# A list scheduler counts all transfers as one pipe instead of fixed landing times

## Chip, cores and metric

The kernel runs on one NeuronCore of one Trainium2 chip. The metric is the device time of one execution in microseconds (us); lower is better. The time before is 2759.6 us, the median of three runs (2759.0 to 2762.83).

## What is computed

The input x holds 32 graphs ("batches") of 512 nodes with 256 features in float32; one 512 x 512 adjacency matrix is shared by all. Four layers follow one another, each a graph attention on a layer-normed input, added to x:

```python
h = relu(layernorm(x)); x = x + elu(gat(h, adj, W0, a0, alpha=0.2))          # layer 0
h = relu(layernorm(x)); x = x + relu(gat(h, adj, W1, a1, alpha=0.01))        # layer 1
h = relu(layernorm(x)); x = x + elu(gat4(h, adj, W2, a2, alpha=0.2))         # layer 2: 4 heads of 64
h = relu(layernorm(x)); x = x + L3(h)                                        # layer 3
...
def gat(h, mask, W, a, alpha):
    v = h @ W
    e = leaky_relu(v @ a1[:, None] + (v @ a2)[None, :], alpha)   # 512 x 512
    return softmax(where(mask, e, -inf)) @ v
...
def L3(h):
    o = relu(h @ mlp1_w + mlp1_b)                     # 512 wide
    o = elu(elu(gat(o, None, W_fc, a_fc, 0.2))) + o   # no mask
    r = relu(o @ mlp2_w + mlp2_b)                     # 256 wide
    return relu(elu(elu(gat(r, adj, W_hand, a_hand, 0.2))) + r)
```

## The kernel before

**Work of one batch.** All 512 nodes of a batch lie on chip as four tiles of 128 rows. A layer norms x (`norm`, L653 to L664, on VectorE/DVE and ScalarE/ACT), transposes the result on TensorE/PE (`turn_pair`, L442; ACT takes it out as hT, L674) and multiplies with the weights (`values`, L434 W,hT). The attention weights are exp of a maximum of two sums, so they are built as a product form: a row of exp terms is brought onto all partitions, and DVE makes each 128 x 512 block of w with one instruction (`weights`, L737: maximum with a column, times the mask). The row goes to DRAM (`rows_out`: PE transpose, ACT copy L749, store "row" L751 on SP's queue) and comes back spread over the partitions (`spread`, L757, 256 KB, three buffers). PE then sums w times v (`aggregate`, L434 v,w), DVE takes a reciprocal (L769), ACT and DVE finish.

Layer 2 has four heads: four spreads, sixteen w, and column-tiled matmuls (L438, three groups of 32 per batch) between transposes. Layer 3 has no mask in its first attention, so for batches 0 to 30 it is computed by sorting (`sort_attend`): DVE and ACT count each node's place (L1003, L1016), POOL writes rows to their places in DRAM with indirect transfers ("order", L1025), SP reads them back ("sums", L1036), DVE and PE make running sums (L1048 to L1070), SP writes them to a table in DRAM (L1071, 1032 KB), and POOL gathers one row per node ("g", L1079); DVE combines them (L1093), ACT and DVE apply elu twice (L1096, L1097, L796 to L798), PE transposes, DVE adds into oT (L1152). The last batch multiplies directly (`attend`). The output is added on POOL (L1137) and stored (L1138).

**Streams.** Four streams (NS = 4) hold batches i, i+4, i+8 and so on. Each is a generator that yields a planner time, `after_us(us)`, which is its step's begin plus STRETCH times the step's PE cycles plus SLOW times the given us. The loop at the end of `fast` always lets the stream with the smallest time go on. Stream i begins at i * LEAD plus an offset; in its first batch it also waits PAUSES[3b + layer] after each of its first three layers. The setup (mask, products of the weights, triangles) is a fifth generator of twelve pieces, written out at a fixed distance. This fixes only the order in which the program is written down, which is each instruction's rank.

**Planner.** The program is built twice. The first time `jobs_of` finds all dependencies, `price` gives each instruction an assumed duration, and `in_order` makes a list schedule: on each engine, of the instructions that are ready by the assumed times, the one of the lowest rank goes next. A tile's buffers and the eight PSUM banks are given out in the same run. The second time the instructions are held in that order on each engine (`arrange`), so an engine whose next instruction waits does nothing else. The assumed durations appear nowhere in the program; the waits on the chip are those of the data.

For a transfer, `price` sets `took` (from issue to landing), `flux` (time in the one shared pipe) and `holds` (the issuing engine). In `in_order` a transfer with a flux is done when the pipe has taken it:

```python
clock[e], done = at + job.holds, at + job.took
if job.flux:
    done = array["pipe"] = max(done, array["pipe"]) + job.flux
```

Before the change only the loads of the kernel's inputs (names that begin with in_) have a flux, at 350 GB/s, x of batches 4 and up excepted. All others land after a fixed time, whatever else is under way: 5.6 us for sums, 4.3 for a spread plus 0.9 for each further head, 6.5 for the table, 6.8 for g, 4.1 for order, 2.6 for a row.

Of the kernel before, what the change touches and what calls it, by code (L numbers as in the profile page):

```python
# [67 lines left out]
class Job:  # L68
# [9 lines left out]
HANDOVER = {"PE": 40.0, "DVE": 33.0, "Activation": 33.0, "Pool": 70.0, "SP": 28.0}  # L78
LANDING = {
    "sums": 5600.0, "spread": 4300.0, "table": 6500.0, "x": 10000.0, "order": 4100.0, "g": 6800.0, "out": 4500.0,  # L80
    "adj": 9000.0,
}
SHORT = {"table": 5200.0, "row": 2600.0, "out": 4500.0}
SWITCH = 93.0
# [25 lines left out]
def price(job, outs, ins, in_psum):  # L110

    e, op = job.engine, job.op
    if op == "Matmult":
        (name, _, moving), (_, _, still) = ins[0], ins[1]
        turned = name.startswith("ident")
        job.span = P if turned else int(job.ins.tile_size[1])
        whole = str(list(job.ins.ins)[1].dtype).endswith("float32")
        job.passes = 2 if whole and not turned else 1
        job.rest, job.fills = [], outs[0][0]
        job.load = 109.0 * elements(still) / P * job.span / P  # L120
        job.flow = 109.0 if turned else (elements(moving) * (5.0 / 6.0 if whole else 0.45) + 2.4) * job.span / P
        return
    n = max(elements(s) for _, _, s in outs + ins) if outs + ins else 1
    wide = [name for name, _, s in ins if elements(s) > 48]
    columns = sum(1 for _, _, s in ins if elements(s) == 1) if n > 48 else 0
    if op == "DMACopy":
        name, _, s = outs[0]
        kind = name.split("_")[0].rstrip("0123456789")
        large = elements(s) * s[0][1] > 5000
        job.took = LANDING.get(kind, 6000.0) if large else SHORT.get(kind, 3300.0)  # L130
        if kind == "spread":
            job.took += 900.0 * (ins[0][1] // 512)
        if ins[0][0].startswith("in_") and not (kind == "x" and ins[0][1] >= 4 * 512 * 256):
            job.took, job.flux = 2500.0, max(160.0, 4.0 * elements(s) * s[0][1] / 350.0)
        job.holds = (2000.0 if kind == "order" else 1290.0) if e == "Pool" else 600.0 if kind in ("sums", "table") else 400.0
        return
    if e == "DVE":
        if op == "BNStats":
            t = 409.0
        elif n <= 48:  # L140
            t = 158.0 + n
        elif op in ("TensorTensor", "TensorReduce") or len(wide) > 1:
            t = 155.0 + 1.042 * n + (55.0 * columns if op == "TensorScalarPtr" else 0.0)
        elif any(map(in_psum, wide)):
            t = 205.0 + 1.045 * n
        else:
            t = 205.0 + 0.43 * n + 45.0 * columns
        job.holds = max(45.0, t - 84.0)
    elif e == "Activation":
        if n <= 48:  # L150
            t = 170.0 + n + 90.0 * (len(ins) > 1)
        elif any(map(in_psum, wide)):
            t = 170.0 + 0.82 * n + 90.0 * min(columns, 1)
        else:
            t = 200.0 + 0.84 * n + 85.0 * min(columns, 1)
        job.holds = max(60.0, t - 100.0)
    else:
        t = 1271.0 if op == "TensorTensor" and n > 48 else 250.0
        job.holds = t
    if len(outs) > 1:  # L160
        job.holds, t = job.holds + 85.0, t + 165.0
    job.took = t
# [238 lines left out]
def fast(ctx, tc, plan, flag, x, adj, w0, a0, w1, a1, w2, a2, mlp1_w, mlp1_b, mlp2_w, mlp2_b,  # L401
# [9 lines left out]
    NS = 4  # L411
    LEAD = 81.69
    GO = 7.0
    PAUSES = (1.98, 20.79, 0, 9.87, 13.42, 5.98, 12.87, 2.43, 0, 28.8, 13.7, 0)
    SLOW = 1.53
    STRETCH = 1.75

# [258 lines left out]
    def turned(xn, when):  # L676
# [4 lines left out]
        turn_pair(xn, hT, 2)  # L681
        yield after_us(0.26)
        return hT
# [8 lines left out]
    def values(hT, w, rs=None):  # L692

        v = work.tile([P, NT, F + 3], FP, tag="v", name="v", bufs=4)
        for t in range(NT):
# [14 lines left out]
            if t + 1 < NT:  # L710
                yield after_us(0.32)
        yield after_us(0.7)
        return v

    def linear_t(inT, w, bias, name, bufs):
# [3 lines left out]
        for f in range(ft):  # L719
# [3 lines left out]
            nc.scalar.activation(o[:, f, :], p, AF.Relu, bias=bias[:, f:f + 1])  # L723
            yield after_us(0.05 if f == ft - 1 else 2.73)
        return o
# [46 lines left out]
    def plain(hT, w, rs=None, far=False):  # L772
        v = yield from values(hT, w, rs)
        r = None
        if far:
            r = spread(rows_out(v[:, :, F + 2], 1)[0, :])
            yield after_us(11.34)
        wt = weights(lambda t: v[:, t, F + 2:F + 3], lambda j: v[:, j, F + 1:F + 2], r=r)
        note(v[:, :, F:])
        yield after_us(0.41)  # L780
        return v, wt
# [18 lines left out]
    def layer0(xt, xn, rs, when):  # L800
        v, wt = yield from plain((yield from turned(xn, when)), W0, far=True)
        xn, rs = new_xn(), small([NT], "rs")
        for t0 in range(0, NT, 2):
            r, q = pair(), pair("q")
            for i in range(2):
# [3 lines left out]
                if i == 0:  # L809
                    yield after_us(0.56)  # L810
            add_elu(xt[:, t0:t0 + 2, :], r, q)
            norm(xt, xn, rs, t0, True)
            last, when = when, after_us(0.48)
            if t0 == 0:
                yield after_us(0)
        yield last
        return xn, rs, when

    def layer1(xt, xn, rs, when):
        v, wt = yield from plain((yield from turned(xn, when)), W1, rs, far=True)  # L820
        xn, rs = new_xn(), small([NT], "rs")
        for t0 in range(0, NT, 2):
            r = pair()
            for i in range(2):
                p, rd = averages(v, wt, t0 + i)
                nc.scalar.activation(r[:, i, :], p, AF.Relu, scale=rd)
                if i == 0:
                    yield after_us(3.06)
            xr = xt[:, t0:t0 + 2, :]
            nc.vector.tensor_tensor(xr, xr, r, op=OP.add)  # L830
            norm(xt, xn, rs, t0, True)
            last, when = when, after_us(1.98)
            if t0 == 0:
                yield after_us(0.04)
        yield last
        return xn, rs, when

    def layer2(xt, xn, rs, when):
        hT = yield from turned(xn, when)
        v = work.tile([P, NT, NH, CH], FP, tag="v", name="v2", bufs=4)  # L840
        for t in range(NT):
# [10 lines left out]
            )  # L852
            yield after_us(1.87 if t + 1 < NT else 0.3)
        row_d = rows_out(v[:, :, :, D + 2], NH)
# [3 lines left out]
        def begin():  # L858
# [3 lines left out]
            )  # L862
            return after_us(0.05)

# [5 lines left out]
        )  # L870
        yield after_us(14.86)
        begin()
        note(v.rearrange("p t h c -> p (t h) c")[:, :, D:])
        yield after_us(0.87)
        when = begin()
        for g, parts in enumerate(plan):
# [9 lines left out]
            nc.scalar.copy(s, p)  # L886
            yield after_us(1.08)
            if g < 2:
# [23 lines left out]
            if g:  # L912
# [3 lines left out]
                add_elu(xt[:, :, (g - 1) * 2 * D:g * 2 * D], y, q)  # L916
            yield after_us(3.1)
        xn, rs = new_xn(), small([NT], "rs")
        for t0 in range(0, NT, 2):
            norm(xt, xn, rs, t0, False)  # L920
        yield after_us(4.83)
        return xn, rs, after_us(1.14)

# [27 lines left out]
    def attend(oT, b):  # L951

        halves, ends = fc_values()
        for c in range(2):
            for t in range(NT):
                project_half(oT, halves, ends, c, t)
                yield after_us(0.48)
            if c == 0:
                nc.gpsimd.tensor_copy(halves[0][:, :, F:], ends[:, :, :2])
                note(ends)  # L960
        wt = weights(lambda t: ends[:, t, 2:3], lambda j: ends[:, j, 1:2], masked=False)
        yield after_us(0.73)
        ys = []
        for t in range(NT):
# [9 lines left out]
            ys.append(y)  # L974
            yield after_us(0.14)
            if t:
                mlp_in(oT, ys[t - 1], t - 1)
                yield after_us(0.1)
        yield after_us(0)
        mlp_in(oT, ys[-1], NT - 1)  # L980
        yield after_us(0)

    def sort_attend(oT, b):
# [6 lines left out]
        for t in range(NT):  # L990
            project_half(oT, halves, ends, 0, t)
            yield after_us(1.43)
        project_half(oT, halves, ends, 1, 0)
        yield after_us(0.78)
        for c in range(2):
            nc.gpsimd.tensor_copy(halves[c][:, :, F:], ends[:, :, :2])
        tj = spread(rows_out(ends[:, :, 1], 1)[0, :])
        yield after_us(5.75)

# [8 lines left out]
        note(ends)  # L1008
        sort = after_us(3.88)
        yield after_us(0.32)  # L1010
        for t in range(1, NT):
            project_half(oT, halves, ends, 1, t)
            yield after_us(3.04)
        for t in range(NT):
# [6 lines left out]
        for c in range(2):  # L1021
# [14 lines left out]
            for read in (nc.sync.dma_start(u, rows), nc.sync.dma_start(flat[c][:, 2, :], rows[:, 0, :])):  # L1036
                for other in placed:
                    tc.add_manual_dep(read.ins, other.ins.name, landed, reason="rows of four tiles")
            sort = after_us(0.46)
        places = table[:N, :].rearrange("(p t) (k c n) -> p (t k) c n", t=NT, k=2, c=2)  # L1040
        sort = after_us(0.54)
        for c in range(2):
# [11 lines left out]
            for t in (2, 1, 0):  # L1054
                nc.vector.scalar_tensor_tensor(  # L1055
                    u[:, t, :], u[:, t, :], T[:, t:t + 1], u[:, t + 1, :], op0=OP.mult, op1=OP.add
                )
            yield after_us(1.92)

# [12 lines left out]
            nc.sync.dma_start(table[N:, c * C:(c + 1) * C], tot[P - 1:, :])  # L1072
            sort = after_us(6.33)
        yield after_us(12.5)
        got, when, gs = [], [], []
# [10 lines left out]
        gather(1)  # L1086
        landed = after_us(9.82)
        for t in range(NT):
# [12 lines left out]
            got.append(y)  # L1101
            landed = after_us(0.46)
            when.append(after_us(12.63))
            if t == 0:
# [4 lines left out]
        mlp_in(oT, got[-1], NT - 1)  # L1109
        yield after_us(0.11)  # L1110

    def layer3(xt, xn, when, b):
# [6 lines left out]
        for t0 in range(0, NT, n):  # L1119
# [21 lines left out]
            if t0 == 0 and b + NS < B:  # L1141
                first_norm(b + NS)
            yield after_us(0)

# [21 lines left out]
    def batch(b):  # L1166
        if b < NS:
            first_norm(b)
            yield after_us(20.8)
        else:  # L1170
            yield after_us(0.8)
        xt, xn, rs = normed.pop(b)
        when = after_us(2.46)
        for i, layer in enumerate((layer0, layer1, layer2)):
# [14 lines left out]

    ready = {i: i * LEAD + late for i, late in enumerate((0, 4.35, 4.97, 5.59))}  # L1190
    streams = [stream(i) for i in range(NS)]
    early = setup()
    ready[NS] = 1.42
    while ready:
        i = min(ready, key=ready.get)
        if i == NS:
            turn[0] = NS - 1
            ready[i] += 19.61
            if next(early, early) is early:
# [463 lines left out]
```

## Time and profile before

| | before |
|---|---|
| runs (us) | 2759.0, 2759.6, 2762.83 |
| profiled execution | 2780.08 us, its span 2778.3 us |
| granted TensorE clock, mean | 0.993 |
| PE, DVE, ACT, POOL busy in the span (us) | 2711.2, 2288.7, 1625.7, 515.4 |
| bytes moved | 314.04 MB, mean 113 GB/s |
| matmuls and weight loads | 13944 each |

The profile is of one execution. Times in it are from the span's start. "A <- B" in the waits means that A was held up until B was done; a chain lists what released what, back from the last instruction. Matmuls overlap one another, so their busy times are those of the union, and the mean of one is longer than its share.

### The profile page before, as it was taken

The page shows a single profiled execution, that of the slowest core. Times are in us where ns is not written, and L with a number is a line of the kernel's source. Part 1 is how long each engine was busy: PE and PEld are TensorE (multiplying, and loading weights), DVE is VectorE, ACT ScalarE, POOL GpSimd, SP SyncE. Part 2 cuts the span into 40 slices and gives each one's busy share as a digit, 9 for nine tenths or more (in the row PEclk, how much of TensorE's full clock was granted, in tenths as well). Part 3 has the DMA queues.
Part 4 walks back from the last instruction along what each step waited for, and adds up shares of the span by engine and source line. Part 5 has one row for each costly group of instructions (what it writes and reads, how often), then busy time and mean ns, then how long its engine had stood idle before and what let it go on. Part 6 is the DMA issues. An engine that isn't in the chain of part 4 may idle for free.

```text
span 2778.3 us, 41413 instructions
## 1 busy us (share of the span) xinstructions
PE 2711.2 (98%) x13944; PEld 1906.2 (69%) x13944; DVE 2288.7 (82%) x5889; ACT 1625.7 (59%) x4228; POOL 515.4 (19%) x516
## 2 busy tenths in 40 slices
PE   5999999999999999999999999999999999999998
PEld 4666677766767676676767667676676766777655
DVE  5788888888878889788897888978989789888875
ACT  3455666566556565555765566655665556565554
POOL 0012221212112221012221222111221112212120
PEclk8999999999999999999999999999999999999999
DMA  4033333334424343144341434423443234333331
GB/s 129 24 103 113 125 122 103 122 107 134 137 77 133 122 132 123 60 136 138 126 134 60 126 131 133 131 69 113 147 136 109 89 115 138 126 102 114 116 131 37
DMA packets 214885, 314.04 MB, mean 113 GB/s; under 512 B 17356, under 2 KB 156934, under 8 KB 214664
## 3 DMA queue, kind: packets, MB, share of 16 engines
q1 hardware_dynamic: 184904, 213.01, 24.8%
q0 software_dynamic: 29760, 98.30, 10.3%
q8 instruction: 112, 1.84, 0.3%
q14 instruction: 109, 0.89, 0.1%
HBM read 195.61 MB, written 115.65 MB: 112 GB/s over the span
## 4 chain that ended last, share of the span: by engine, by line
PE 69%; DVE 23%; ACT 5%; issue 1%; DMA 1%; SPq 0%; another core or an unknown queue 0%; DVEq 0%
PE b L434 54%; PE b L438 8%; PE b L442 7%; DVE w L737 6%; DVE st L653 2%; DVE sums L1055 1%; DVE y L798 1%; DVE xn L664 1%; DVE sums L1070 1%; DVE xn L660 1%; DVE y L1134 1%; ACT q L797 1%; DVE sums L1063 1%; DVE y L791 1%; DVE g L1093 1%
## 5 line engine op out<-in xcount | busy, mean ns | idle before, releaser
L434 PE MATMUL b<-v,w 128*128 128x257 f32 (+1 forms) x3136 | 756.5, 382 | 16.8 <-DVE w L737 14.8
L434 PEld LDWEIGHTS b<-v,w 128*128 128x128 f32 x3136 | 576.8, 190 | 141.9 <-issue 30.6
L737 DVE SCALAR_TENSOR_TENSOR w<-spread,v,maskT 128x512 f32<-128x512 f32 x896 | 651.7, 760 | 26.1 <-DMA spread<-row 26.1
L434 PE MATMUL b<-WFC,oT 128*128 128x256 f32 (+1 forms) x2048 | 504.7, 381 | 0.0
L434 PEld LDWEIGHTS b<-WFC,oT 128*128 128x128 f32 x2048 | 373.2, 189 | 79.3 <-issue 26.1
L434 PE MATMUL b<-W,hT 128*128 128x259 f32 (+1 forms) x1536 | 387.2, 388 | 0.8 <-ACT hT L674 0.8
L1025 POOL DMA_INDIRECT order<-v,at x248 | 264.1, 1065 | 628.3 <-DVE w L737 194.7
L438 PE MATMUL b<-w,v 128*32 128x512 f32 x3072 | 349.5, 595 | 0.0
L434 PEld LDWEIGHTS b<-W,hT 128*128 128x128 f32 x1536 | 277.5, 192 | 56.5 <-issue 12.0
L1079 POOL DMA_INDIRECT g<-table,at x124 | 137.9, 1112 | 889.4 <-DMA table<-sums 194.8
L434 PE MATMUL b<-hT,WM 128*128 128x512 f32 x512 | 239.8, 593 | 1.2 <-ACT hT L674 1.2
L434 PE MATMUL b<-oT,WM 128*128 128x512 f32 x512 | 234.8, 603 | 4.7 <-DVE oT L1152 4.7
L438 PEld LDWEIGHTS b<-w,v 128*32 128x32 f32 x3072 | 89.9, 109 | 196.4 <-issue 196.0
L653 DVE BATCH_NORM_STATS2 st<-x 128x6 f32<-128x256 f32 x512 | 193.3, 408 | 5.5 <-DMA x<-in_x_dram 3.4
L798 DVE TENSOR_TENSOR y<-q,y 128x512 f32<-128x512 f32 (+1 forms) x194 | 135.7, 700 | 57.3 <-ACT q L797 48.8
L442 PE MATMUL b<-ident,xn 128*128 128x128 f32 x1024 | 163.4, 280 | 17.9 <-DVE xn L660 6.8
L442 PEld LDWEIGHTS b<-ident,xn 128*128 128x128 f32 x1024 | 121.7, 141 | 72.0 <-DVE xn L664 15.3
L434 PEld LDWEIGHTS b<-oT,WM 128*128 128x128 f32 x512 | 98.4, 193 | 105.5 <-issue 96.7
L674 ACT ACTIVATE hT<-b 128x512 f32<-128x512 f32 x256 | 150.5, 592 | 26.1 <-PE b L442 25.1
L949 ACT ACTIVATE v<-b,ends 128x256 f32<-128x256 f32 x256 | 119.6, 471 | 66.6 <-PE b L434 62.4
L769 DVE RECIPROCAL rden<-b 128x1 f32<-128x1 f32 x388 | 59.2, 161 | 118.9 <-PE b L434 116.0
L1137 POOL TENSOR_TENSOR x<-x,y 128x512 f32<-128x512 f32 x62 | 86.3, 1392 | 368.9 <-ACT y L1135 365.0
(145 smaller groups left out, 4028.0 us busy)
## 6 DMA issues: line engine op xcount, KB each, us to landing
spread<-row SPq DMA_DIRECT2D x255, 256.0 KB
table<-sums SPq DMA_DIRECT2D x62, 1032.0 KB
sums<-order SPq DMA_DIRECT2D x62, 516.0 KB
x<-in_x_dram SPq DMA_DIRECT2D x32, 512.0 KB
out_dram<-x SPq DMA_DIRECT2D x62, 256.0 KB
sums<-order SPq DMA_DIRECT2D x62, 129.0 KB
order<-v,at POOLq DMA_INDIRECT x248
row<-row SPq DMA_DIRECT2D x127, 2.0 KB
```

What stands on the lines that cost most here:

```text
L434: nc.tensor.matmul(p, w, x, **flags)
L438: nc.tensor.matmul(p, w, x, tile_position=(0, c), **flags)
L442: nc.tensor.transpose(p, x, i)
L653: nc.vector.bn_stats(st[:, i, :], xt[:, t0 + i, :])
L674: nc.scalar.activation(hT[:, :, t0 * P:(t0 + 2) * P], p.rearrange("p (k n) -> p k n", k=KF), AF.Relu)
L737: nc.vector.scalar_tensor_tensor(wt[:, j, :], r, t_col(j), maskT[:, j, :], op0=OP.max, op1=OP.mult)
L769: nc.vector.reciprocal(r, den)
L798: nc.vector.tensor_tensor(r, q, r, op=OP.add)
L949: nc.scalar.activation(halves[c][:, t, :F], ps[:, :F], AF.Copy, scale=ends[:, t, 0:1])
L1025: one = nc.gpsimd.indirect_dma_start(out=orders[c], out_offset=bass.IndirectOffsetOnAxis(ap=at[:, 0, t:t + 1], axis=0), in_=halves[c][:, t ...
L1079: nc.gpsimd.indirect_dma_start(out=g, out_offset=None, in_=table, in_offset=bass.IndirectOffsetOnAxis(ap=at[:, 1, t:t + 1], axis=0),)
L1137: (nc.gpsimd if n == 2 else nc.vector).tensor_tensor(xr, xr, y, op=OP.add)
```

## The change

In `price` every transfer gets a flux: its bytes over RATE = 300 GB/s (for an order transfer a fixed 132096 bytes), and a shorter `took` that stands before it. The per-head term of the spread goes. Input loads keep 2.5 us and a flux of 0.86 times that, about 350 GB/s as before. Beside this all the numbers that set the streams' planner times are given new values. The instructions themselves, their shapes, the buffers and the queues are not touched.

```diff
-LANDING = {
-    "sums": 5600.0, "spread": 4300.0, "table": 6500.0, "x": 10000.0, "order": 4100.0, "g": 6800.0, "out": 4500.0,
-    "adj": 9000.0,
-}
-SHORT = {"table": 5200.0, "row": 2600.0, "out": 4500.0}
+LANDING = {"sums": 2800.0, "spread": 2800.0, "table": 3000.0, "x": 6000.0, "order": 3300.0, "g": 3900.0, "out": 1900.0, "row": 2300.0}
+RATE = 300.0
...
         kind = name.split("_")[0].rstrip("0123456789")
-        large = elements(s) * s[0][1] > 5000
-        job.took = LANDING.get(kind, 6000.0) if large else SHORT.get(kind, 3300.0)
-        if kind == "spread":
-            job.took += 900.0 * (ins[0][1] // 512)
+        job.flux = (132096.0 if kind == "order" else 4.0 * elements(s) * s[0][1]) / RATE
+        job.took = LANDING.get(kind, 2500.0)
         if ins[0][0].startswith("in_") and not (kind == "x" and ins[0][1] >= 4 * 512 * 256):
-            job.took, job.flux = 2500.0, max(160.0, 4.0 * elements(s) * s[0][1] / 350.0)
+            job.took = 2500.0
+            job.flux = max(160.0, 0.86 * job.flux)
...
-    LEAD = 81.69
+    LEAD = 81.07
     GO = 7.0
-    PAUSES = (1.98, 20.79, 0, 9.87, 13.42, 5.98, 12.87, 2.43, 0, 28.8, 13.7, 0)
-    SLOW = 1.53
-    STRETCH = 1.75
+    PAUSES = (51.06, 25.58, 4.03, 0.47, 3.65, 0, 0, 0.28, 19.16, 14.86, 15.77, 8.83)
+    SLOW = 1.52
+    STRETCH = 1.72
...
         if b < NS:
             first_norm(b)
-            yield after_us(20.8)
+            yield after_us(7.32)
         else:
-            yield after_us(0.8)
+            yield after_us(0)
...
-    ready = {i: i * LEAD + late for i, late in enumerate((0, 4.35, 4.97, 5.59))}
+    ready = {i: i * LEAD + late for i, late in enumerate((0, 9.28, 13.52, 23.24))}
...
-    ready[NS] = 1.42
+    ready[NS] = 3
...
             turn[0] = NS - 1
-            ready[i] += 19.61
+            ready[i] += 2.1077082524068596
```

Some forty further delays inside the layers change in the same way. Those of over one planner-us, in the order of the code: after `values` 0.7 to 2.1; after layer 0's second pair 0.48 to 2.74; within layer 1's pairs 3.06 to 2.02; between layer 2's values 1.87 to 0.66 and after them 0.3 to 3.2; before its first weights 14.86 to 17.41, after them 0.87 to 2.11; after each of its groups 3.1 to 0.58; after its norm 1.14 to 3.09; in `sort_attend` before the spread 0.78 to 2.41, after it 5.75 to 9.61, before the order transfers 3.88 to 6.59, before and between the later half's projections 0.32 to 3.14 and 3.04 to 4.59, before the running sums 0.54 to 2.62, between their parts 1.92 to 0.29, after the first half 6.33 to 0, after the gathers 9.82 to 17.6, before the adding into oT 12.63 to 10.07, at the end 0.11 to 5.55.

## Prediction

> **What bounds the kernel now.** I read the engine shares first, then a table by stage, then the waits of PE and DVE, then the chain at the start.
>
> ```profile
> PE 2711.2 (98%) x13944; PEld 1906.2 (69%) x13944; DVE 2288.7 (82%) x5889; ACT 1625.7 (59%) x4228; POOL 515.4 (19%) x516
> PE 69%; DVE 23%; ACT 5%; issue 1%; DMA 1%; SPq 0%; another core or an unknown queue 0%; DVEq 0%
> ```
>
> TensorE (PE) is busy for 2711.2 of 2778.3 us, and transfers own 1% of the chain that ended last. So 67.1 us of PE idle time is nearly all that an order can win, and a transfer counts only where it keeps PE waiting. The table by stage shows where those 67 us lie (PE, PEld, DVE, ACT and POOL busy, then clock, DMA share, GB/s):
>
> ```profile
> 0.00:25.00 25.00, 12.58 (x53) 10.23 (x53) 11.96 (x39) 8.97 (x22) 1.69 (x10) 1.00 0.95 302
> 25.00:60.00 35.00, 20.53 (x81) 16.33 (x81) 21.87 (x95) 11.78 (x36) 2.36 (x6) 0.76 0.11 33
> 60.00:112.00 52.00, 45.16 (x255) 30.13 (x256) 39.31 (x105) 20.61 (x60) 1.52 (x3) 0.97 0.10 36
> 112.00:335.00 223.00, 216.76 (x1130) 149.49 (x1130) 179.44 (x479) 124.79 (x328) 39.35 (x40) 0.99 0.31 99
> ...
> 443.05:778.00 334.95, 334.04 (x1733) 235.33 (x1733) 284.47 (x729) 202.65 (x529) 64.97 (x64) 1.00 0.37 118
> ...
> 2650.00:2700.00 50.00, 45.48 (x199) 28.95 (x198) 34.57 (x83) 28.03 (x66) 11.91 (x12) 0.93 0.40 131
> 2700.00:2778.30 78.30, 64.93 (x287) 48.55 (x285) 41.43 (x90) 39.88 (x92) 8.01 (x7) 0.96 0.14 47
> ```
>
> Idle PE: 12.4 + 14.5 + 6.8 = 33.7 us before 112 us, 6.2 up to 335, 17.9 after 2650. In between the kernel repeats a pattern of 335 to 336 us (four batches) in which PE idles 0.9 to 1.9 us: 8.3 us over the six repeats from 443 to 2457. The start and the end hold 58 of the 67 us.
>
> What the start waits for (us in total, times, longest), and the chain there (start, us, what):
>
> ```profile
> PE b L434 <- DVE w L737: 13.1, 2, 12.1
> PE b L442 <- DVE xn L660: 4.4, 2, 3.7
> PE b L442 <- ACT rs L656: 3.5, 1, 3.5
> ```
>
> ```profile
> 26.93 3.52 DMA row<-row
> 30.47 3.05 DMA spread<-row
> 33.55 0.76 DVE w L737
> ...
> 56.07 1.30 DMA row<-row
> 57.39 3.07 DMA spread<-row
> ```
>
> PE waits 12.1 us for the first weights w, which wait for a row that goes out to DRAM and comes back spread over the partitions. With 302 GB/s of setup loads just ended the row takes 3.52 us, without them 1.30.
>
> **Part 1, the planner's transfers.** Nothing that computes is added or removed: 13944 matmuls before and after, the same transfers and waits. Only the order on each engine and the PSUM banks differ. Planned landings go down: the spread from 4.3 us (5.2, 6.1 and 7.0 for layer 2's later heads) to 2.8 + 262144/300 ns = 3.7; sums from 5.6 to 4.6; the gather g from 6.8 to 5.7; order from 4.1 to 3.7; x from 10 to 7.7; table stays at 6.5. The trace's landing records give medians of 3.3 (spread), 4.0 (sums), 5.3 (g), 3.7 (order), 4.1 (x), 5.4 (table). The new figures are nearer in all that moved and still not below the medians, so consumers planned on them should seldom come too early on an idle pipe. And a spread issued within 5 us after a table write lands in 6.35 us (7 cases, median) against 3.27 with nothing large ahead: the single pipe would see that, the old plan did not.
>
> What this is worth once the pattern runs: DVE's idle time that transfers ended is 26.1 us (spread, 20 times, longest 7.2, and that at the start), 5.3 (g) and 3.7, of 490 us idle in all; PE is 99.6% busy meanwhile. Better landings there buy almost nothing directly. What they change is the pattern. Bounds per 335 us: all 0.9 to 1.9 us of idle gone, or a share of idle like that of the unsettled stretch 112:335, 6.2/223 = 2.8% against 0.4%. Over the 2207 us from 443 to 2650 that is -8 to +53. Nearest rows are the six repeats of a pattern from the same kind of planner; I take **-3**.
>
> The start is different: the old plan lets row and spread pass beside the setup loads, the new one puts them behind them in the pipe. It can then see the hole from 22.2 to 34.4 us and lay other work in. Batch 1's x was issued at 3.4 us; its norm costs DVE 4 x (0.41 + 0.17) + 4 x 0.41 = 4.0 us and fits in the 7.2 us that DVE idles there; it frees 8 transposes and 16 matmuls of W,hT, 8 x 0.16 + 16 x 0.25 = 5.3 us of PE. Bounds: 0 if nothing is laid in, -12 if the hole closes; I take **-5** for one batch.
>
> The Trainium skill speaks against the one pipe: "DMA: Bandwidth & Descriptors", section "Queues, rings and completion order", has each DMA engine take turns between its queues packet by packet, so a transfer of SP's queue doesn't stand behind one of POOL's. The records agree for two queues: a spread after a gather lands in 3.55 us against 3.27 alone, where the pipe would add up to 528384/300 ns = 1.8 us. By that rule the plan is up to 1.8 us late behind gathers, and the sum would be the same -3, since a late plan costs nothing while PE has other work.
>
> **Part 2, the constants.** Setup pieces are written out every 2.1 planner-us instead of 19.6, so twelve of them rank in by 28 rather than 237. They hold some 16 us of DVE work (16 L522 on WFC 6.7, its reads 1.3, the L522, L614 and L615 of the other weights 6.8, ties and bands 1.4). In the trace much of it already runs in the hole. Ranked first it can push batch 1's norm out (+5) or free later DVE time (PE's 4.4 and 3.5 us of waits for xn and rs at 44 and 82): -6 to +5, taken as **-1**.
>
> The pauses change the streams' distances. Start, offset and three pauses give, in planner-us, stream 0 to 3 at 35, 131, 192, 316 before (0 + 1.53 x 22.8; 86.0 + 1.53 x 29.3; 168.4 + 1.53 x 15.3; 250.7 + 1.53 x 42.5) and 123, 97, 205, 326 after (1.52 x 80.7; 90.4 + 1.52 x 4.1; 175.7 + 1.52 x 19.4; 266.4 + 1.52 x 39.5). The last two streams stay 124 and 121 apart, so the end keeps its form. Its 17.9 us of idle are handovers of DVE and ACT (the largest, PE for y L798, 4.1 us). Bounds: -8 (about half goes, as batches end nearer together) to +8; taken as **-4**. Streams 0 and 1, 96 apart before, are now 26 apart and swapped: the main risk, below. The other delays of layers and sort rank work within a stream; they are part of the pattern's -3.
>
> **Sum.** -3 - 5 - 1 - 4 = -13 us on a span of 2778.3 (the profiled execution took 2780.08, 20.5 above the median of the runs, 2759.6). I carry the difference over: span 2765, and 2759.6 - 13 = 2746.6, said as **2746**.
>
> **Rivals.**
> 1. Slower: two streams in step make VectorE the bound in layer 2. Per batch layer 2 costs DVE 16 x 0.745 (w) + 4 x 0.48 (v) + 1.8 (y) + 0.7 (rden) + 2 x 1.37 (L791, L792) + 3.9 (norm) = 23 us, but PE 4.0 + 10.9 + 8 x 0.16 + 12 x 0.146 = 18. Alone, another stream's matmuls fill the 5 us; with two in step DVE owes 10 us and the other two streams must have that ready. For: already DVE is full in some slices:
>
> ```profile
> 1550.88:1567.66 16.78, 16.78 (x95) 12.92 (x97) 16.55 (x43) 11.04 (x31) 3.80 (x5) 1.00 0.49 152
> 1618.02:1634.81 16.79, 16.78 (x89) 13.95 (x91) 16.71 (x36) 11.45 (x31) 4.51 (x4) 1.00 0.52 171
> ```
>
> Against: PE lost nothing there, since layer 3 of a stream brings more PE than DVE work. Price: 5 us a round not covered, 8 rounds, 40 us; half covered, +20. With the start's gain kept (-5) half of the time: 2767 to 2795, say 2779. It decides once a round loses more than (13 + 5.5)/8 = 2.3 us.
> 2. The change doesn't do what it says: transfers end 1% of the chain, the new order packs PE as tightly as the old, and the hole stays because the setup work fills DVE. 2754 to 2765, say 2760.
> 3. The start is packed throughout: the hole (-12), the waits for xn and rs (-8), the end -8, the pattern -5: 2727.
>
> **How the numbers follow.** Forecast (2735 to 2754) 0.45; rival 3 (2715 to 2735) 0.06; rival 2 0.13; rival 1 0.36, of which 0.12 beyond 2786. The bound between them is 0.2%, 5.5 us, about what a measurement of this kernel can tell from no change. So faster 0.51, same 0.13, slower 0.36. The range 2728 to 2786 leaves out about 0.03 below and 0.12 above. The cases of both signs are close; the likeliest one's own range is 2735 to 2754.
>
> **What would show it.** Right: PE's wait for w near 22 us falls from 12.1 to under 8; PE idle before 112 us falls from 33.7 to about 28; the repeats stay at 334 to 336 us with PE idle below 2; the end idles about 14 us. Wrong: a repeat of 338 us or more with PE waiting for w L737 or spread (rival 1), or no repeat at all; the hole unchanged (rival 2). DVE's waits for spread growing well over 26 us would say that the landings are planned too short, which the medians above speak against.

## The result and the profile after

The changed kernel takes 2749.5 us (median of six runs, 2746.2 to 2752.1) against 2761.0 (2758.7 to 2763.2) for the kernel before beside it: a ratio of 0.9953, 95% interval 0.9943 to 0.9963. By the ratio that is 13 us less (the two medians differ by 11.5). Its profiled execution took 2749.5 us with a span of 2747.2.

The profile of before that the prediction used was of one execution 20 us above that kernel's median. The kernel before was run again as a control (first experiment); its profiled execution took 2760.7 us, span 2758.5, which is near the median, so from here on the profile after is set against the control. Line numbers after are 4 lower: L430 is L434, L733 is L737.

Engine shares and the chain's shares, control first, then after:

```profile
PE 2701.5 (98%) x13944; PEld 1907.7 (69%) x13944; DVE 2288.5 (83%) x5889; ACT 1625.5 (59%) x4228; POOL 511.7 (19%) x516
PE 68%; DVE 24%; ACT 5%; issue 1%; DMA 1%; SPq 0%; POOL 0%; DVEq 0%; POOLq 0%
```

```profile
PE 2692.0 (98%) x13944; PEld 1915.6 (70%) x13944; DVE 2265.5 (82%) x5889; ACT 1637.1 (60%) x4228; POOL 536.0 (20%) x516
PE 85%; DVE 11%; DMA 2%; ACT 1%; issue 1%; SPq 0%; DVEq 0%; ACTq 0%
```

The span is 11.3 us shorter, and 9.5 of these went out of PE's busy time; its idle time fell only from 57.0 to 55.2 us. So what the order won is hardly visible as idle time. One execution can differ from another of the same program by as much: PE was busy 2711.2 us in the profile of before that the prediction read, 2701.5 in the control, 2692.0 after and 2694.8 in a second profile of the changed kernel (e10 below). The table by stage (PE, PEld, DVE, ACT, POOL busy, clock, DMA share, GB/s), control and after:

```profile
0.00:60.00 60.00, 32.42 (x135) 25.78 (x135) 34.35 (x135) 21.10 (x60) 4.00 (x16) 0.83 0.47 145
60.00:112.00 52.00, 45.74 (x258) 30.78 (x259) 39.60 (x107) 20.00 (x58) 1.52 (x3) 0.97 0.11 36
444.00:778.00 334.00, 333.43 (x1734) 235.82 (x1733) 284.13 (x728) 202.68 (x529) 64.43 (x64) 1.00 0.37 118
2680.00:2758.50 78.50, 65.16 (x288) 48.79 (x286) 41.55 (x90) 40.23 (x93) 8.01 (x7) 0.98 0.15 48
```

```profile
0.00:25.00 25.00, 11.37 (x53) 9.10 (x53) 17.36 (x59) 8.68 (x22) 3.73 (x15) 0.97 0.96 305
25.00:60.00 35.00, 22.82 (x81) 17.98 (x81) 19.25 (x80) 11.98 (x36) 1.37 (x4) 0.68 0.08 23
60.00:112.00 52.00, 43.82 (x240) 30.86 (x244) 38.43 (x103) 20.00 (x61) 0.00 (x0) 0.97 0.12 41
766.30:1099.50 333.20, 332.52 (x1733) 236.83 (x1733) 281.27 (x729) 204.00 (x529) 68.40 (x65) 1.00 0.37 118
2669.00:2747.20 78.20, 65.42 (x296) 49.74 (x294) 42.32 (x96) 44.21 (x97) 9.80 (x8) 0.96 0.18 58
```

Before 112 us PE idles 27.6 + 6.3 = 33.8 us in the control and 13.6 + 12.2 + 8.2 = 34.0 after: the start won nothing. A repeat of the pattern takes 333.0 to 333.8 us instead of 333.9 to 335, with the idle time of PE as small as before.

Each batch's last store of its output marks the stages without any window to choose (us, from the trace; in brackets the changed kernel's second profile, taken later on a chip where the kernel before took 2772 us, 9 more than beside the control, so that the differences in brackets may be too high by some us):

| | control | after | difference |
|---|---|---|---|
| start, to batch 6's store | 767.5 | 766.3 (769.2) | -1.2 (+1.7) |
| five repeats, to batch 26's store | 1671.7 | 1666.2 (1667.7) | -5.5 (-4.0) |
| end, to batch 31's store | 314.7 | 309.8 (310.3) | -4.9 (-4.4) |

What the start waits for, PE's waits before 112 us, after:

```profile
PE b L430 <- DVE w L733: 19.1, 3, 13.5
PE b L438 <- ACT rs L652: 4.0, 2, 2.7
PE b L438 <- DVE xn L656: 1.1, 1, 1.1
```

The first line was 15.8 us, at most 14.6, in the control. The chain there, after:

```profile
15.49 9.31 DMA WHA<-in_L_gnn_W_hand_dram
...
24.86 3.09 DMA row<-row
27.97 3.29 DMA spread<-row
31.29 0.76 DVE w L733
```

And what DVE did meanwhile (two of 16 such pieces, the last of them, and the first w):

```profile
22.64 0.43 DVE L518 SCALAR_TENSOR_TENSOR junk<-WFC,vectors 128x256 bf16<-128x256 f32 x1
23.11 0.42 DVE L518 SCALAR_TENSOR_TENSOR junk<-WFC,vectors 128x256 bf16<-128x256 f32 x1
...
30.02 0.42 DVE L518 SCALAR_TENSOR_TENSOR junk<-WFC,vectors 128x256 bf16<-128x256 f32 x1
30.37 0.08 DVE L518 DVE_READ_ACCUMULATOR junk<-WFC,vectors 128x1 f32 x1
31.29 0.75 DVE L733 SCALAR_TENSOR_TENSOR w<-spread,v,maskT 128x512 f32<-128x512 f32 x1 [0.84 <-DMA spread<-row]
```

DVE's wait just before the first w went from 7.4 us in the control to 0.8, and its idle time in the whole of PE's hole from 11.0 to 2.1: the setup work that now ranks first fills it. None of it gives PE anything to do, so PE's hole stayed.

At the end, PE's waits in the last 125 us, control and after:

```profile
PE b L442 <- DVE y L798: 3.6, 3, 1.8
PE b L434 <- DVE w L737: 1.7, 2, 1.1
PE b L434 <- DVE oT L1152: 1.3, 3, 0.8
```

```profile
PE b L430 <- DVE w L733: 1.3, 1, 1.3
PE b L430 <- DVE w L737: 0.9, 1, 0.9
```

The wait for y (L794 after) is gone; PE idles 13.4 us there (13.1 in the second profile) instead of 17.0.

### The profile page after: what moved, and what is told of

It reads as the page before. It is cut to its first block, busy times and chain, and to the rows that moved or that the text cites. A ratio compares the mean times of both kernels' runs of the same rounds, so it can differ in the third digit from the quotient of the medians.

```text
span 2747.2 us, 41511 instructions
## 1 busy us (share of the span) xinstructions
PE 2692.0 (98%) x13944; PEld 1915.6 (70%) x13944; DVE 2265.5 (82%) x5889; ACT 1637.1 (60%) x4228; POOL 536.0 (20%) x516
## 4 chain that ended last, share of the span: by engine, by line
PE 85%; DVE 11%; DMA 2%; ACT 1%; issue 1%; SPq 0%; DVEq 0%; ACTq 0%
PE b L430 67%; PE b L434 10%; PE b L438 8%; DVE w L733 3%; DVE st L649 1%; DVE y L794 1%; DMA spread<-row 1%; DVE sums L1051 0%; DVE q L792 0%; DVE g L1089 0%; DVE xn L656 0%; DVE y L1130 0%; DVE parts L931 0%; DMA WHA<-in_L_gnn_W_hand_dram 0%; DVE sums L1059 0%
## 5 line engine op out<-in xcount | busy, mean ns | idle before, releaser
L430 PE MATMUL b<-v,w 128*128 128x257 f32 (+1 forms) x3136 | 743.3, 383 | 23.1 <-DVE w L733 22.2
L430 PEld LDWEIGHTS b<-v,w 128*128 128x128 f32 x3136 | 585.5, 191 | 147.1 <-issue 32.7
L733 DVE SCALAR_TENSOR_TENSOR w<-spread,v,maskT 128x512 f32<-128x512 f32 x896 | 645.8, 753 | 23.9 <-DMA spread<-row 21.8
L430 PE MATMUL b<-WFC,oT 128*128 128x256 f32 (+1 forms) x2048 | 506.7, 381 | 0.0
L430 PEld LDWEIGHTS b<-WFC,oT 128*128 128x128 f32 x2048 | 371.3, 190 | 76.9 <-issue 28.1
L1021 POOL DMA_INDIRECT order<-v,at x248 | 273.0, 1101 | 635.2 <-DVE at L1003 220.2
L430 PE MATMUL b<-W,hT 128*128 128x259 f32 (+1 forms) x1536 | 380.8, 387 | 0.9 <-ACT hT L670 0.8
L434 PE MATMUL b<-w,v 128*32 128x512 f32 x3072 | 349.4, 595 | 0.0
L430 PEld LDWEIGHTS b<-W,hT 128*128 128x128 f32 x1536 | 278.5, 191 | 58.6 <-issue 12.3
L430 PE MATMUL b<-hT,WM 128*128 128x512 f32 x512 | 239.2, 593 | 0.7 <-ACT hT L670 0.4
L430 PE MATMUL b<-oT,WM 128*128 128x512 f32 x512 | 233.7, 593 | 0.8 <-DVE oT L1148 0.8
L434 PEld LDWEIGHTS b<-w,v 128*32 128x32 f32 x3072 | 89.9, 109 | 193.1 <-issue 190.3
L438 PE MATMUL b<-ident,xn 128*128 128x128 f32 x1024 | 154.3, 277 | 6.0 <-ACT rs L652 4.0
L794 DVE TENSOR_TENSOR y<-q,y 128x512 f32<-128x512 f32 (+1 forms) x194 | 132.7, 684 | 32.2 <-ACT q L793 30.0
L430 PEld LDWEIGHTS b<-oT,WM 128*128 128x128 f32 x512 | 96.5, 190 | 88.0 <-issue 82.5
L793 ACT ACTIVATE q<-q,minus 128x512 f32<-128x512 f32 (+1 forms) x194 | 138.6, 715 | 22.3 <-DVE q L792 20.1
L652 ACT ACTIVATE rs<-mv,eps 128x2 f32<-128x2 f32 x256 | 75.0, 293 | 127.8 <-DVE mv L650 125.9
```

The costliest lines, as they stand in the source:

```text
L430: nc.tensor.matmul(p, w, x, **flags)
L434: nc.tensor.matmul(p, w, x, tile_position=(0, c), **flags)
L438: nc.tensor.transpose(p, x, i)
L652: nc.scalar.activation(rp, mv[:, :, 1], AF.Ln, bias=eps)
L733: nc.vector.scalar_tensor_tensor(wt[:, j, :], r, t_col(j), maskT[:, j, :], op0=OP.max, op1=OP.mult)
L793: nc.scalar.activation(q, q, AF.Exp, bias=minus1)
```

## Experiments

The question was where the 13 us come from. Three theories: the truer count of the transfers makes the better order; the new numbers make it, whatever the count; or neither does alone, because the numbers were fitted to one count. For the start: SP's queue holds the row back, DVE's setup work keeps batch 1 out, or the loads themselves are in the way. Every kernel was timed in five rounds against the kernel before beside it.

| | ratio to before | a repeat, us | PE idle in the pattern, us | DVE's wait for spread in L733, us |
|---|---|---|---|---|
| control | 1.0004 (0.9995 to 1.0013) | 333.9 to 335 | 4.4 | 26.5 |
| after | 0.9953 (0.9943 to 0.9963) | 333.0 to 333.8 | 5.6 | 21.8 |
| e2 transfers only | 1.0261 (1.0243 to 1.0278) | 342.4 to 344 | 41.0 | 49.8 |
| e3 numbers only | 1.0123 (1.0108 to 1.0139) | 337 to 341 | 23.5 | 17.3 |
| e4 no pipe | 1.0120 (1.0104 to 1.0135) | 337 to 340 | 32.4 | 41.0 |
| e7 rate 295 | 1.0090 (1.0077 to 1.0103) | 339 to 341 | 37.2 | 34.5 |
| e7 rate 320 | 1.0010 (1.0001 to 1.0019) | 335 to 338 | 17.6 | 44.4 |
| e11 rate 295, re-chosen | 0.9983 (0.9974 to 0.9992) | 335 to 338 | 12.4 | 46.1 |
| after again (e10) | 0.9930 (0.9916 to 0.9943) | 333 to 334 | 6.9 | 29.6 |

"In the pattern" is from 443 us to 125 us before the end. There the granted clock was 1.00 throughout in the control and in both profiles of the changed kernel. The other orders of the table show between one (e2) and four (e4 and rate 295) stretches of 3.4 us at about half the clock; by our estimate, at half speed throughout them, these cost e4 at most 7 of its 33 us, and none of the others more.

The sets of runs were on several chips. The changed kernel stands at 0.9953 in one set and at 0.9930 in another, and the two intervals only meet at their edges: ratios of different sets can differ by some 0.2% more than an interval says.

**e1_control.** The kernel before, unchanged.

> The kernel before, unchanged, once more. Every theory expects 1.000 times the time before, and a second profile of it: the profiled execution of before stood 20 us above the median of the runs (2780 against 2760). If that was a freak of one execution, this profile has a span near 2758 us, and the repeats of the pattern are 333 to 334 us instead of 335 to 336 (theory P: part of the difference of the two traces is the profile's). If the repeats stay at 335 to 336 us and the span near 2778, the profiler itself costs this order 20 us.

1.0004. Its profile is shown above. The 20 us of the profile that the prediction read belong to that execution (or to its chip, which the record does not name), not to profiling as such: repeats of 335 to 336 us there, 333.9 to 335 here, with the same mean clock within 0.001.

**e2_planner_only.** The kernel before with the new count of the transfers and the old numbers:

```diff
-        job.took = LANDING.get(kind, 6000.0) if large else SHORT.get(kind, 3300.0)
+        job.flux = (132096.0 if kind == "order" else 4.0 * elements(s) * s[0][1]) / RATE
+        job.took = LANDING.get(kind, 2500.0)
```

> The kernel before with the new transfer model alone (one pipe, shorter landings), all planner times of the streams as before. Theory A (the nearer landings and the pipe give the gain): 0.993 to 0.998. Theory B (the gain is that of numbers chosen together; either half alone is just another order): 1.000 to 1.015, with repeats of 335 us or longer. Theory C (the transfer model counts for nothing): 0.998 to 1.002 with nearly the same repeats.

1.0261, above the 1.015 that theory B allowed: the new count alone makes the kernel 70 us slower. One repeat by its window, then PE's waits from 443 to 2630 us:

```profile
782.00:1124.40 342.40, 336.12 (x1733) 235.84 (x1733) 284.19 (x730) 202.49 (x529) 64.59 (x64) 1.00 0.36 115
```

```profile
PE b L430 <- DVE oT L1148: 8.4, 12, 0.8
PE b L438 <- DVE xn L660: 8.0, 12, 0.8
PE b L438 <- ACT y L1120: 5.0, 6, 0.8
PE b L430 <- ACT hT L670: 4.2, 6, 0.7
```

Such waits came 6 or 12 times, that is once or twice in each of six repeats: one order, repeated, with small gaps at many places, not one broken stage. PE's busy time rises too, 336.1 in a repeat against 332.5.

**e3_consts_only.** The changed kernel with the old count (the first lines of the change's diff taken back), the new numbers kept.

> The changed kernel with the old transfer model: fixed landings, new planner times of the streams. Theory A: 0.999 to 1.01 of before, since the gain is in the model. Theory B: 1.000 to 1.015, repeats of 335 us or longer. Theory C: as the changed kernel, 0.993 to 0.998.

1.0123, 35 us slower than before. PE's longest sum of waits from 443 to 2630 us:

```profile
PE b L434 <- DVE w L737: 18.9, 12, 2.8
```

So each half of the change alone costs, 70 and 35 us, and the two together gain 13. The theories of one half (A and C) fall.

**e4_no_pipe.** The changed kernel in which each transfer takes as long as before on an idle pipe, but does not wait for another one (the input loads, which shared a pipe before the change too, stay in it):

```diff
+        else:
+            job.took, job.flux = job.took + job.flux, 0.0
```

> The changed kernel, but transfers other than the first loads land a fixed time after their issue, equal to what the new model gives on an idle pipe (spread 3.7 us, sums 4.6, g 5.7, table 6.5): the shorter landings without the queueing. If the pipe itself is what counts (theory A, narrow), 0.998 to 1.01 of before and more waits of DVE for spread and g. If the shorter landings count, 0.993 to 0.998. If any change of the plan moves the time (theory B), 0.997 to 1.01 with no link to the waits for transfers.

1.0120, above the 1.01 that both theories had as their upper end. The sizes of the landings are those of the changed kernel; only the queueing is gone, and the whole gain with it. That doesn't show that the queueing is the truer picture: the numbers were chosen with it in the count, and the next two kernels lose the gain with the queueing in place. PE's waits from 443 to 2630 us (lines are 2 higher than after):

```profile
PE b L440 <- DVE y L796: 12.4, 8, 2.0
PE b L432 <- DVE w L735: 10.5, 12, 1.1
PE b L432 <- ACT y L1122: 3.2, 6, 0.7
```

**e7_rate_295 and e7_rate_320.** One number of the count, `RATE`, 1.7% lower or 6.7% higher:

```diff
-RATE = 300.0
+RATE = 295.0
```

> The changed kernel with 295 GB/s for the pipe instead of 300: a transfer of 256 KB takes 15 ns more in the plan. As a picture of the chip it is as good. If the gain comes from a truer picture (theory A), 0.993 to 0.998 of before. If it comes from delays chosen to fit one exact plan (theory B), 0.998 to 1.012, with a pattern of its own.

> The changed kernel with 320 GB/s for the pipe. Theory A: 0.993 to 0.998 of before. Theory B: 0.993 to 1.012, another pattern; a time as good as the change's is possible but then with other repeats.

1.0090 and 1.0010. The trace can't say which of 295, 300 and 320 is true: a transfer of 256 KB differs by 0.015 us between the first two, while the landings of the 256 KB spreads after range from 3.0 to 6.8 us. Yet 295 costs more than the change gains. At 295, PE's waits from 443 to 2630 us:

```profile
PE b L430 <- DVE w L733: 11.2, 6, 3.1
PE b L438 <- DVE y L794: 10.5, 6, 1.8
PE b L438 <- DVE xn L660: 6.4, 5, 1.3
```

The times are not even in order with the rate. That is what one would expect of a fitted order, in which a small nudge changes which of two ready instructions goes first and the rest follows from there; the steps between were not traced.

**e11_rate_295_rechosen.** Rate 295, and eight of the numbers that set the streams' times chosen anew for it (the expectation counted nine), by trial in the planner's own reckoning; three of them:

```diff
-    PAUSES = (51.06, 25.58, 4.03, 0.47, 3.65, 0, 0, 0.28, 19.16, 14.86, 15.77, 8.83)
+    PAUSES = (51.06, 25.58, 4.03, 0.47, 3.65, 0.0, 0.0, 0.28, 19.16, 12.3243, 15.77, 5.8588)
...
-            yield after_us(0.66 if t + 1 < NT else 3.2)
+            yield after_us(0.66 if t + 1 < NT else 2.3823)
```

> The kernel with the pipe at 295 GB/s that stood at 1.009, with nine of its planner times chosen anew by trial for a shorter schedule in the planner's own reckoning (no chip in the loop). Theory B (what counts is that the numbers are chosen for the very model in use): most of the loss goes, 0.994 to 1.003, repeats back to 333 to 336 us from 339 to 341. Theory A (300 GB/s is the truer picture) or a loss that has nothing to do with the choice: it stays at 1.005 to 1.012.

0.9983, beside 0.9930 for the changed kernel on the same chip. Of about 1.5% between the changed kernel and 1.0090 (of another set), 1.1% came back, by numbers alone and with a count that is no truer. The repeats, 335 to 338 us, stayed above the forecast 333 to 336. PE's one large wait in the pattern is now:

```profile
PE b L438 <- DVE y L794: 9.9, 6, 2.0
```

**e10_after_again.** The changed kernel beside e11 and e12.

> The changed kernel, unchanged, once more, so that the next two have it beside them on the same chip. Every theory expects 0.995 of before, with repeats of 333 us.

0.9930 (0.9916 to 0.9943); its stages are in brackets in the table of stores.

**e6_setup_slow.** The setup's pieces at the old distance:

```diff
-            ready[i] += 2.1077082524068596
+            ready[i] += 19.61
```

> The changed kernel with the setup's pieces written down 19.6 planner-us apart as before. If the early rank of the setup is what keeps the first hole of PE open (13.5 us after the change, 12.1 before), the hole shrinks by up to 5 us and the start with it: 0.993 to 0.995 of before. If the setup's rank only trades places, the start stays and the pattern too: 0.994 to 0.997. If any change of a number gives back what the numbers together gain, 0.998 to 1.01 through another pattern.

0.9945 (0.9932 to 0.9958), the same as the changed kernel within the intervals. The hole is 13.2 us, so the setup's rank isn't what holds it open; PE's idle time before 112 us is 37.4, against 34.0 and 35.0 in the changed kernel's two profiles, and batch 6's store comes at 770.4, against 766.3 and 769.2. By these single profiles the earlier setup is worth 1 to 4 us at the start.

**e8_row_first.** On SP's queue, the small loads and table stores that stood between the setup loads and the first row are put behind its spread; on DVE, the setup work on WFC and WHA behind the first four w:

```diff
+    late = [j for i, j in enumerate(line[:row]) if out(j, "bias", "table") or out(j, "x_") and i > 20]
+    order["SP"] = [j for j in line[:after] if j not in late] + late + line[after:]
...
+    late = [j for j in line if out(j, "WFC", "WHA", "dots")]
```

> The changed kernel with two orders altered by hand at the start, all the rest of the plan kept: on SP's queue the biases, the table's zero rows and the fifth x go behind the first row and its spread; on DVE the setup work on WFC and WHA goes behind the first four w, one piece after each other instruction. If the first hole of PE is made by SP's queue (the row copied at 18.9 us goes out at 24.9), the first w comes 4 to 5 us earlier, the hole falls from 13.5 to about 9 us, and the time is 0.993 to 0.994 of before. If the setup loads hold the row up on the way in any case, the hole stays over 12 us and the time is 0.995 to 0.997.

0.9964 (0.9952 to 0.9976). The chain at the start (lines are 27 higher than after):

```profile
19.84 6.99 DMA row<-row
26.84 3.06 DMA spread<-row
29.93 0.76 DVE w L760
```

The row goes out 5.0 us earlier than after (24.86) and lands 1.1 us earlier (26.83 against 27.95): it waited in the queue instead of in front of it. PE's hole is 11.6 us, between the two forecasts (about 9, over 12), so the row's place on SP is a small part of the cause. The setup work, now laid between the pieces of batch 0's next norm, delays that (PE's waits for its xn, L683 here, are 9.5 us, 4.8 at most, against 1.1 for L656 after).

**e9_loads_later.** As e8, but the loads of layer 3's weights (WFC and WM alone are four of 512 KB) also go behind the first spread, and DVE's setup work starts later:

```diff
+    late = [j for i, j in enumerate(line[:row]) if any(n.startswith("in_L3") for n in names(j)) or out(j, "table") or out(j, "x_") and i > 20]
```

> The changed kernel with the start altered by hand: on SP's queue all loads that only layer 3 needs (about 3.9 MB), the table's zero rows and the fifth x go behind the first row and its spread; on DVE the setup work on WFC and WHA goes behind the first thirty instructions after the first w, one piece after each other instruction. If the row waits because the loads fill the pipe ahead of it (26.84 us whether it is issued at 19.8 or 24.9), its landing now falls to about 21 us, the first w comes near 24 instead of 31.3, PE's wait for it falls from 13.5 to about 6 us, and the time to 0.991 to 0.993 of before. If something else holds PE there, or later norms and the moved DVE work take the place of the wait, 0.994 to 0.998 with PE idle before 112 us still over 32.

0.9939 (0.9925 to 0.9953). The chain at the start, and PE's wait before 112 us:

```profile
18.67 1.18 DMA row<-row
19.86 4.42 DMA spread<-row
24.31 0.76 DVE w L760
```

```profile
PE b L457 <- DVE w L760: 12.3, 3, 6.8
```

The hole is halved, 13.5 to 6.8 us, PE's idle time before 112 us falls from 34.0 to 28.6, and batch 6's store comes at 763.1 instead of 766.3. The loads were the cause: from e8 to e9 the row's way from issue to landing fell from 6.99 to 1.18 us. The time stayed above the 0.991 to 0.993 forecast for this case. Of the 5 us, about 3 last to the end of the span (2744.4 against 2747.2), which the timed ratios of separate sets (0.9939, and 0.9953 and 0.9930 for the changed kernel) can't separate from nothing.

**e12_loads_later_rechosen.** e9 with eight of the numbers chosen anew for it in the planner's reckoning (two of the pauses 19.16 to 11.94 and 14.86 to 12.31, six smaller changes; the expectation counted seven).

> The kernel with layer 3's loads behind the first row (0.9939), with seven planner times chosen anew in the same way under the 300 GB/s model. If the choice by the planner's reckoning carries over to the chip, 0.990 to 0.994 and faster than the changed kernel beside it by 4 to 8 us; if the plan's last microseconds mean nothing on the chip, 0.994 to 1.000, with another pattern.

0.9931 (0.9918 to 0.9945), beside 0.9930 for the changed kernel: no gain. The start keeps its 28.9 us of idle time, batch 6's store comes at 767.1, and the pattern gives the gain back: repeats of 333.5 to 336 us and 9.3 us of PE idle. In this one trial the planner's last microseconds did not carry over to the chip.

## Why the prediction was right, and where it was wrong

The time (2746 against 2749.5) and the sum (-13 against -13 by the ratio, -11.3 between the spans of control and after) hold. The terms do not all: the start gave next to nothing of its 6 us and the pattern gave more than its 3. That the sum comes out is partly luck, since these two misses cancel.

**The hole of the start, -5: this step failed.** "It can then see the hole from 22.2 to 34.4 us and lay other work in"; batch 1's norm "fits in". The planner did lay work in, and DVE's wait before the first w fell from 7.4 to 0.8 us, but it was the setup's work, and PE's hole stayed (13.5 us against 14.6). The prediction had named that as the +5 of its next term and then counted the two as if they were independent. It is also what rival 2 said of the hole, though that rival's time (2754 to 2765) did not come. The setup's rank is not the whole reason, though: with the rank taken back (e6) the norm didn't come either. In the profiles of the control, after, e6, e8 and e9, batch 1's four statistics run right behind the four of batch 0's second norm, which need the late w. After, DVE's statistics in the first 60 us:

```profile
6.24 0.39 DVE L649 BATCH_NORM_STATS2 st<-x 128x6 f32<-128x256 f32 x1
...
42.64 0.75 DVE L649 BATCH_NORM_STATS2 st<-x 128x6 f32<-128x256 f32 x2
45.28 0.75 DVE L649 BATCH_NORM_STATS2 st<-x 128x6 f32<-128x256 f32 x2
46.03 0.40 DVE L649 BATCH_NORM_STATS2 st<-x 128x6 f32<-128x256 f32 x1
```

The first two lines after the gap are batch 0's second norm; batch 1's begins at 46.03. The code has a reason for it. `jobs_of` lets a tile be opened only behind the one of the same tag that was written down before it (L217 to L219 after):

```python
if (pool, tag) in newest:
    mine[0].soft.add(newest[pool, tag])
newest[pool, tag] = mine[0]
```

Batch 0's second norm is written before batch 1's first, both use the tags xn, st, mv and rs, so with the norms written in this order batch 1's could not go into the hole by any price of a transfer. All traces agree with that; a kernel that writes batch 1's norm earlier was not run, so it is read, not shown. The prediction priced what fits into a hole and did not read what may go there.

**The setup's rank, -1** with bounds -6 to +5: e6 puts it at -1 to -4 (batch 6's store at 770.4 without, 766.3 and 769.2 with). With the hole's 0 the start as a whole is -1.2 and +1.7 in two profiles, against -6 forecast.

**The pattern, -3:** right in sign and too small. Five repeats give -5.5 and -4.0, so over the 6.6 repeats from 443 to 2650 some -5 to -7. The prediction said that "67.1 us of PE idle time is nearly all that an order can win". That was wrong as a way to read the page: the idle time in the pattern went from 4.4 to 5.6 us and the repeat still became 1.1 us shorter (mean of five).

The rest can be counted from each matmul's start to the next one's in the trace, less what its shape takes undisturbed (transposes 0.109 us, full matmuls of 256 to 268 columns 0.215 to 0.226, of 512 columns 0.429, four column-tiled ones together 0.429, one of the running sums 0.118). By this count a repeat holds 7.7 us of small interruptions in the control, idle time included, and 6.7 after (7.0 in the second profile). 2.5 of it in both are the 24 changes between layer 2's column-tiled matmuls and full ones. What fell are the changes between transposes and matmuls (135 to 118 of them, 1.2 to 0.7 us), gaps between transposes (1.0 to 0.5) and between matmuls (1.9 to 1.6), while the running sums' rose (0.8 to 1.1). The slow kernels show the same measure: 16.3 us with the transfers only, 12.0 with the numbers only, 13.6 at 295. In the profile of before that the prediction read, whose order is the control's, it is 9.3: a difference of 1.6 us can come from the execution, and these 1.0 us, unlike the timed ratio, are not clear of that.

**The landings "buy almost nothing directly":** held. DVE's wait for spread fell by 4.7 us and the second profile has 29.6, more than the control's 26.5, at a shorter time; at 295 re-chosen it is 46.1 at 0.9983, and with the numbers only it is 17.3 at 1.0123. It doesn't order the kernels at all, so it is no sign of a good or bad order here.

**The end, -4:** right, -4.9 and -4.4 (some 0.6 of it the pattern's). The waits for y that it named go, the last four batches end nearer together (batch 28's store to the last one 131.1 us in the control, 121.2 after), and the idle time falls from 17.0 to 13.4 us, forecast 14. The size was a choice between two bounds, not worked out, so that it came this near is luck in part.

**Rival 1, streams in step:** did not come in the changed kernel. Repeats are 333.2 us, DVE is busy 281 us in each against 284, and PE waits for w L733 in the pattern 1.8 us in all. The distances that the prediction worked out from the delays (streams 0 and 1 at 96 before, 26 after) did not foretell the chip's: the outputs of the four batches of a repeat follow one another at 72, 77, 76 and 109 us in the control and at 76, 70, 77 and 110 after. The risk itself was real: e2, e3, e4 and e7 show orders of the same planner that cost up to 70 us, more than the bound of +53. The sign of rival 1, repeats of about 338 us with PE waiting for w, does stand in e3, where the same numbers meet the old count (18.9 us of waits for w in the pattern). So it isn't the pauses alone that decide this, as the prediction had assumed; what the runs show is a misfit between the numbers and the count.

**The pipe itself:** it is right where the loads are. The row behind the setup loads took 6.99 us from issue (e8) against 1.18 without them (e9). The Trainium skill, "DMA: Bandwidth & Descriptors", section "Two DMAs through the same engine are not ordered", says that within one queue of one DMA engine descriptors start in order, and these two rows agree with it.

Between queues the prediction weighed the section "Queues, rings and completion order" (turns, packet by packet) against the row of 3.55 us behind a gather. That row mixes near and far: before, the 12 spreads issued within 3 us of a gather landed in 4.1 us (median). After, the 27 issued within 5 us of one (and not behind a table store) landed in 4.1 us against 3.3 for those behind neither: 0.8 us more, between none and the 1.8 us of the pipe. The measurement decides, and neither picture fits it alone. The row of 6.35 us behind a table write is also narrower than it was put: before, 15 spreads were issued within 5 us of one, of which the 7 issued 0.6 us after it took 6.35 us (median) and the 8 issued about 4.6 us after it took 3.1.

**What stays open.** Whether a truer count makes good numbers easier to find, or any count would do after as much fitting, isn't settled. e11 had eight numbers chosen anew, by a short search, and still lacks 0.5%. The old count with numbers chosen anew for it as long as for the new one was not run; as good a time there would mean that the new count itself is worth nothing.

## What to carry to other kernels

In a list-scheduled kernel the cost model and the delays are one fitted set: judge a change of the model only with delays chosen for it. Here a change of 1.7% in one assumed rate moved the time by 1.4%, more than the whole change won. Before pricing work into a hole, read what the scheduler allows there (order of buffers, ranks) and whether the engine that waits gets anything from it. And judge a full engine by the start-to-start time of its instructions, not by its idle time: between the two profiles here nine of eleven microseconds won were inside the busy time.

## What the runs showed of the hardware that was not expected

- A row of 2 KB that took 1.18 us from issue to landing on a quiet queue (e9, 2 GB/s moving) took 6.99 us behind the setup loads (e8, 300 GB/s before it and 237 while it waited). Issuing it 5.0 us earlier brought it 1.1 us.
- A spread of 256 KB landed in 3.3 us with no table store or gather in the 5 us before it (median), in 6.35 when issued 0.6 us after a table store of 1 MB (before, 7 cases), in 3.1 when issued 4.6 us after one (before, 8 cases), and in 5.9 for the 40 issued within 5 us of one after, most of them within 3.
- The 24 changes per repeat between column-tiled (128 x 32) and full matmuls cost 2.5 to 2.7 us in every kernel measured, some 0.10 us each (0.09 on the way in, 0.11 on the way out), whatever the order.
- The same program took 2760.7 and 2780.1 us in two profiled executions at a granted clock of 0.994 and 0.993, and its median was 2763, 2767 and 2772 us in sets of runs on three chips. Within a set a kernel's times lie within some 0.4% of one another, so only ratios to a kernel beside it mean something here.
- Where the mean granted clock of one kernel's executions differs, the time goes with it: five executions of the transfers-only kernel at 0.991, 0.991, 0.990, 0.989 and 0.987 took 2829.9, 2831.8, 2833.1, 2836.2 and 2841.9 us.
